# Another order table for the 6,604 calls of a cross-attention kernel

## The chip, the core and the metric

The kernel runs on one core of a Trainium2 chip. Its engines are TensorE (PE; PEld is its weight load), VectorE (DVE), ScalarE (ACT), GpSimd (POOL) and SyncE (SP), which here only issues transfers. The metric is the device time of one execution in microseconds; the median of a few runs is given.

## The reference

Eight batches of 256 rows of width 1024 attend to a context of 256 rows, which serves as keys and as values, with 32 heads of width 32. Everything is float32.

```python
x = (hidden_states - mu) * jax.lax.rsqrt(var + LN_EPS) * ln_gamma + ln_beta
Q = _split_heads(x @ Wq.T)
K = _split_heads(memory_keys)
V = _split_heads(memory_values)
scores = jnp.einsum('bhsd,bhtd->bhst', Q, K) * scale
scores = jnp.where(mask, scores, -jnp.inf)
probs = jax.nn.softmax(scores, axis=-1)
attn = jnp.einsum('bhst,bhtd->bhsd', probs, V)
out = attn.transpose(0, 2, 1, 3).reshape(B, S, HIDDEN) @ Wout.T
return residual + out
```

## The kernel before, in words

**The steps.** Four heads of one batch make a step, so there are 64 steps, n = 0 to 63, eight to a batch. Step n goes through every engine:

- `scores(n)`: 8 matmul calls on PE (tiles `sc`), from the queries (`qa`, `qlo` or a part of `ring`) and the keys `k`. The PSUM pool has four buffers for `sc`, so scores n wait for VectorE to have read scores n-1.
- `softmax_parts(n)`: VectorE adds the mask and takes the minimum (8 calls, tile `e` from `sc`), ScalarE takes the exponentials (8 calls, with the sums `den`), VectorE the reciprocals `rden`; GpSimd, for some tiles ScalarE, scales `e` by them; VectorE transposes four tiles in 32x32 blocks into `pT`. ScalarE copies a part of `pT` aside into `pc`.
- the swaps (`tail` and `swap` in the same function): two transfers `pT<-pT` and then two `pT<-pc`, 128 KB each, put the blocks of partitions in place. SP issues them.
- `values(n)`: 32 matmul calls into `pv`, from `pT` and the values `v_all`. For n = 8 to 53 `values_pair` does two steps at once, 64 calls in a row. In the tables of the profile `pv` is the tile's name.

A matmul call in float32 is two weight loads and two matmuls in PE's stream. So a pair of value runs is 256 instructions, and its matmuls are short: 32 columns of weights on 128.

**The projections.** Between these, PE works on the query projection of a later batch (`pq`; with fewer products of half blocks, `pq_b_P1` to `P7`, for the batches 2 and 3, 4 and 5, 6 and 7) and on the output projection of an earlier one (`po_A`, `po_S`, one product for each of `A11`, `A12`, `A22`, `S1` to `S4`). Sums of weights that those need are kept in DRAM (`kept_T1`, `kept_T3`, `kept_B11`, `kept_B21`) and read back into `ring` or `wq`. `x` is normalized into `xe` and moved in blocks into `xnT`; `r` is the residual. `v_all` has one buffer, `k` two.

**What sets the order.** No scheduler does. The code of `xattn_kernel` is run once against a stand-in, `Recorded` (lines 351 to 371), which writes down each of its 6,604 calls with its engine. Then `nc.issue(ORDER, OTHER)` (line 1606) makes the calls in the sequence that the string `ORDER` (lines 151 to 321) lists by number. Each engine's queue is its own calls in that sequence, and a queue is in order: a call that waits holds everything behind it on its engine. So every instruction in the profile has the line of the call in `issue`, line 367 here, and it is told apart by its tiles. Semaphore waits follow from the data; a PE run placed earlier or later in `ORDER` meets other calls ahead of it, and nothing else changes.

The first transfers stand at the head of SP's queue: `x_0` in four pieces, the slices of `wq` (512 KB each), `x_1` in two (512 KB each), `k`, the mask, `wo` and `v_all`.

Of the kernel before, what the change touches and what calls it, by code (L numbers as in the profile page):

```python
# [151 lines left out]
0-38 41 39-40 47 44 42-43 48 54-57 81 58-77 80 83-88 78-79 94 89-92 95-109 120-123 134 133 93 135 111 110  # L152
112-113 124-130 136-137 114 131 118-119 115-116 138-141 148 142-146 149 147 150-153 156 160-161 132 157 167
158 179-180 162-165 117 159 172 177 181 166 184 168 174 169 176 175 186-187 178 170 182 185 82 171 209 154-155
173 183 189-196 217 188 215-216 223 225 213-214 226 224 218 231 236 229-230 227 237 239 234 287-288 232-233
388 50 45-46 49 197-199 205 200-202 210 203-204 238 228 235 254-261 211 206 212 247 262 207 263-264 274 208
275 265-266 276 488 52 51 219-220 518 243 598 221-222 748 241 240 248 244-246 293-294 250 252 251 280-281 242
249 270 291 253 297-298 278 282 292 279 283 302 295 299 301 300 322 267 277 315 296 323 271 268-269 306 324
328-330 419 307-309 304-305 303 311-314 327 326 331-335 325 372 272 368 273 369 373 370 374-375 371 376-379
414 425 318 320 319 382-383 380-381 310 316-317 336-367 384 321 385 394 396-397 395 400-401 426-427 402-403  # L160
407 398-399 408 411 405-406 409 393 392 410 413 412 404 416 418 417 420 415 422 424 428-430 1236 284-286 53
290 289 421 423 431-478 481 487 387 386 389 391 390 496-497 479-480 482-483 498-499 492 505 500-501 484
506-507 493-495 502 504 503 509 513 515-516 508 517 536-576 581 531-534 582 577 583-585 578 597 486 485 623
510-512 514 524 591-592 521 523 525-526 529 589-590 522 527 519-520 530 611-612 535 593-594 609 605-606
613-614 607 603-604 608 610 615-617 602 601 628 620 625 624 631 641 622 627 621 633 626 632 643-650 579-580
586-588 691-693 619 629 634 694-695 699 635 528 491 490 596 595 489 630 651-690 696 704 709-710 703 705-707
711-712 708 716 718 713-715 725 721 727 618 726 720 719 717 749-756 1235 737 599-600 757-788 741 852 700 697
738 698 850 734 637 809 914 851 702 701 854 636 853 855 735 1598 639 722-723 728 724 747 640 745 793-794
742-744 795-796 789-792 797-800 816-817 801 803 730 733 813 732 731 802 804 820 814-815 805 812 818 821-825
819 826 834 831 827-828 806 729 807 736 638 808 829 836-837 833 832 838-839 642 849 810 739-740 856-897 845  # L170
842-843 830 835 840-841 844 848 898-901 908 906-907 846-847 909 923 938 921-922 919 910 924-925 911-912 811
920 917 926-927 943 930 935 949 932-933 918 931 950 940 953 962-963 746 928-929 937 936 939 941-942 944 946
951 948 947 964 966 902-905 974-981 967-969 1014-1017 982-1013 1028 1032-1035 952 954 1029 965 1038 1036
1026-1027 934 1030 1039 1037 955 1045-1046 945 1043-1044 1047 1040 1055 1050 1068 913 958 915 1079-1086 1166
916 957 1385 970 1018-1025 1048 1042 1049 1041 971 1056 1052-1053 1031 1051 1054 1058 1063 1077 1087-1121
1126-1127 1134 1132-1133 1062 1123 1122 1128 1061 1131 1135 1057 1130 1138 1178-1180 1059-1060 1244 1240 1173
1175 1074 1171 961 1461 1668 1064-1065 1067 956 1072 1066 1129 1136 1139 1137 1148 1143-1144 1140 1142
1145-1147 1149-1150 1141 1152-1155 1151 1157 1160-1161 1073 960 1070 1169 1158-1159 1078 972 1181-1186 1124
1187-1189 1125 1176 1190-1194 1245 1069 1234 1071 1237 959 1460 1199 1197-1198 1200 1203 1195-1196 1162
1205-1207 1209 1212 1201-1202 1210 1228 1211 1213 1204 1156 1251-1322 1387 1208 1218 1215 1217 1216 1177 1224  # L180
1226 1225 973 1335-1336 1214 1323-1326 1337 1219 1221-1222 1163 1165 1164 1220 1241 1167-1168 1243 1338 1340
1345-1346 1229 1327-1329 1343-1344 1227 1349-1353 1223 1230-1231 1233 1232 1359-1361 1247 1356 1347-1348
1354-1355 1357-1358 1362 1366 1374 1242 1379 1239 1238 1388-1395 1330-1334 1383 1396-1398 1407 1368 1370 1369
1372 1408 1373 1367 1399-1406 1413 1363-1365 1249 1248 1250 1667 1375 1371 1376 1378 1409-1410 1415-1416 1446
1377 1172 1449 1424 1419-1421 1411-1412 1417-1418 1414 1450 1422-1423 1341 1425 1451 1430 1427 1431 1426 1433
1342 1432 1339 1436 1440 1437 1441 1438 1452 1463-1536 1588 1439 1592 1174 1170 1381 1596 1428-1429 1434-1435
1459 1386 1454-1455 1462 1246 1545-1546 1553-1554 1551 1442 1543-1544 1555-1556 1552 1564-1565 1443 1557-1563
1566 1568 1567 1457 1456 1589 1569-1573 1547 1575 1577 1576 1593 1599-1606 1537-1542 1594-1595 1607-1608
1621-1622 1549 1578 1625 1619 1627 1617 1582 1634 1623 1636 1632 1665 1865 1380 1445 1444 1382 1574 1580-1581
1448 1447 1579 1609-1613 1618 1620 1624 1635 1626 1633 1628 1583 1638-1639 1076 1640 1663 1629 1642 1644 1550  # L190
1643 1548 1647-1648 1650 1645 1666 1649 1664 1458 1660 1741 1614-1616 1652 1631 1669-1740 1742-1744 1765-1766
1630 1651 1745-1749 1761-1763 1653 1641 1646 1764 1654 1767 1774 1753-1754 1590 1768 1776-1778 1591 1597
1755-1756 1758 1780 1772-1773 1775 1661 1782 1769-1771 1785 1787 1779 1808-1815 1750-1752 1802-1804 1816
1827-1828 1789 1788 1825-1826 1760 1829 1791 1793 1817-1820 1837-1838 1869-1870 1662 1584-1585 1453 1586 1657
1655-1656 1075 1587 1784 1783 1384 1786 1757 1790 1792 1794-1796 1659 1658 1833-1834 1830 1842 1831-1832
1843-1844 1839 1846 1840 1835-1836 1759 1841 1849 1864 1798 1845 1797 1637 1879 1871-1878 1821-1824 1880-1882
2009 1807 1799-1800 1805 1847-1848 1853 1855 1957 1959-1961 1955 1850 1852 1956 1962 1851 1958 1854 2010 1857
1806 1856 1859-1860 1947-1949 1979 1858 1861 1863 1862 1965 1963-1964 1971-1973 1966-1967 1868 1970 1974 1983
1801 1988 2011-2018 1883-1946 1950-1952 1978 1994 1867 1866 1781 2002 2006-2007 1953-1954 2218 2224 2076 1980
1999 1968 1984 1969 1982 1985 1989-1990 1981 2028-2030 1976 1995 2045-2046 1986 2031 1975 1977 1987 1993 1992  # L200
2008 2019 2034 2042 1991 1996-1997 2040 2044 2005 2043 2047-2048 2032-2033 2038 2041 2039 2035 2052-2053 2072
2054-2055 2079-2150 2020-2023 2161 2163-2164 2049 2036-2037 1998 2051 2050 2061 2058 2070-2071 2024-2027 2078
2060 2059 2075 2151-2152 2162 2177 2175-2176 2056 2167 2171-2172 2179 2000 2178 2207 2063-2064 2173-2174 2057
2065 2003 2067 2001 2004 2066 2180 2169-2170 2188 2062 2153-2154 2185 2182-2183 2181 2187 2186 2189 2191-2192
2184 2190 2074 2073 2199 2225-2232 2155-2158 2219-2220 2159-2160 2233-2234 2247 2197 2243 2249-2250 2281
2068-2069 2285 2251-2252 2168 2194 2196 2195 2206 2244 2248 2253-2254 2208 2200 2245-2246 2193 2198 2201 2166
2165 2209 2222 2077 2235-2242 2284 2267 2255 2262 2260 2263 2258 2269 2261 2259 2272 2288-2290 2217 2256-2257
2265-2266 2268 2274 2264 2276 2275 2270 2292 2216 2303-2374 2297 2376-2381 2384 2394-2395 2271 2434 2273 2277
2386-2387 2385 2392-2393 2390 2278 2396 2398-2399 2389 2403-2404 2400 2402 2407-2409 2223 2286 2300 2302 2405
2287 2299 2414 2435-2442 2382-2383 2375 2431 2455-2457 2401 2397 2420 2411-2412 2406 2413 2416-2417 2410 2419  # L210
2428 2418 2433 2301 2221 2443-2444 2432 2445-2450 2453 2458 2454 2429 2461 2470 2422 2451-2452 2462 2468-2469
2472 2466 2459 2474 2485 2463-2464 2473 2465 2298 2497-2499 2574-2575 2573 2501-2508 2576-2581 2626 2211 2210
2202 2491 2291 2295 2421 2212 2204 2215 2280 2214 2296 2294 2203 2293 2213 2494 2479 2496 2475 2687 2490 2279
# [1433 lines left out]
```

## Time and profile before

| | us |
|---|---|
| median of 3 runs | 572.59 (571.46 to 572.81) |
| the profiled execution's own time | 572.86 |
| its span, first to last instruction | 571.1 |
| PE busy | 559.8 |
| VectorE, ScalarE, GpSimd busy | 463.8, 441.4, 402.5 |
| mean granted TensorE clock | 0.997 |

How to read the profile: a row of the timeline is a run of like instructions, with its start and its length in us, and in brackets the idle time before it with what ended that. In a row of windows stands, behind the stretch and its length, the busy time and the count of instructions of PE, PEld, DVE, ACT and POOL, then the granted clock, the share of the DMA engines and GB/s. A group's row ends in its busy time, the mean in ns of one, and the idle time before its instructions. "issue" is idle time that ended on nothing that the profile shows. The DMA queue q8 carries TensorE's instructions; q1 the transfers that SP issues.

### The profile page before, as it was taken

What the parts mean: (1) busy time and instruction counts of PE and PEld (TensorE: products, weight loads), DVE (VectorE), ACT (ScalarE), POOL (GpSimd) and SP (SyncE); (2) the same over time, 40 slices, a digit from 0 to 9 for tenths busy, and PEclk for the clock granted to TensorE, in tenths of its full rate; (3) what the DMA queues carried; (4) which work ended last, traced back from release to release, by engine and by line L of the source; (5) the groups of instructions that cost most, each with busy time, mean ns of one, the idle gap of its engine ahead of it and who ended that gap; (6) DMA issues with size and microseconds to landing.
All of it is one profiled execution on the core that took longest, in us unless ns stands there. A gap on an engine that the chain in (4) does not pass through costs nothing.

```text
span 571.1 us, 18695 instructions
## 1 busy us (share of the span) xinstructions
PE 559.8 (98%) x6586; PEld 374.2 (66%) x6586; DVE 463.8 (81%) x1709; ACT 441.4 (77%) x1475; POOL 402.5 (70%) x633
## 2 busy tenths in 40 slices
PE   8999999999999999999999989999999999899997
PEld 7787776676666766767666656666766666555544
DVE  6799898898798979887898958887777788788824
ACT  3599998798886687978877858887869758898930
POOL 1579898989978684679967783378865776366781
PEclk9999999999999999999999989999999999999999
DMA  8988874887567877877667767687665755665443
GB/s 303 365 229 235 232 196 112 223 245 222 166 183 232 222 200 207 226 211 200 174 174 228 207 177 225 167 232 190 170 176 152 208 152 145 190 200 142 131 113 129
DMA packets 46477, 112.64 MB, mean 197 GB/s; under 512 B 9008, under 2 KB 9776, under 8 KB 46384
## 3 DMA queue, kind: packets, MB, share of 16 engines
q1 hardware_dynamic: 40384, 91.52, 56.7%
q0 software_dynamic: 5712, 19.93, 11.6%
q8 instruction: 52, 0.85, 0.6%
q14 instruction: 41, 0.34, 0.2%
q10 hardware_dynamic: 288, 0.01, 0.0%
HBM read 58.99 MB, written 12.58 MB: 125 GB/s over the span
## 4 chain that ended last, share of the span: by engine, by line
PE 88%; DMA 4%; DVE 3%; ACT 3%; issue 1%; SPq 0%; ACTq 0%; DVEq 0%
PE pq_P L367 25%; PE po_S L367 19%; PE sc L367 11%; PE pv L367 11%; PE po_A L367 10%; PE pq L367 8%; PE po_end L367 3%; ACT e L367 2%; DMA wq<-in_wq_dram 2%; PE po_last L367 1%; DMA pT<-pc 1%; DVE e L367 1%; DMA pT<-pT 1%; DVE pT L367 1%; DMA bet<-in_beta_dram 1%
## 5 line engine op out<-in xcount | busy, mean ns | idle before, releaser
L367 ACT ACTIVATE e<-e,mn 128x256 f32<-128x256 f32 x512 | 255.8, 501 | 53.7 <-DVE mn L367 44.0
L367 POOL TENSOR_SCALAR e<-e,rden 128x256 f32<-128x256 f32 x408 | 190.4, 480 | 127.7 <-DVE rden L367 119.4
L367 DVE CUSTOM_DVE_ANT_0 e<-sc,mb 128x256 f32<-128x256 f32 x512 | 191.7, 411 | 12.8 <-PE sc L367 9.5
L367 DVE STREAM_TRANSPOSE pT<-e 128x512 f32<-128x512 f32 x256 | 175.2, 699 | 30.1 <-POOL e L367 21.2
L367 PE MATMUL pq_P<-xnT,wq 128*128 128x256 f32 x544 | 133.4, 386 | 2.7 <-issue 2.6
L367 PEld LDWEIGHTS pq_P<-xnT,wq 128*128 128x128 f32 x544 | 102.0, 191 | 45.2 <-issue 29.9
L367 ACT ACTIVATION_READ_ACCUMULATOR e<-e,mn 128x1 f32 x512 | 96.9, 189 | 0.0
L367 ACT COPY pc<-pT 128x512 f32<-128x512 f32 x128 | 76.9, 611 | 15.1 <-DVE pT L367 9.6
L367 PE MATMUL po_S<-wo,at 128*128 128x512 f32 x152 | 73.1, 603 | 0.0
L367 DVE RECIPROCAL rden<-den 128x2 f32<-128x2 f32 x256 | 37.4, 153 | 34.2 <-ACT e L367 32.5
L367 PE MATMUL pv<-pT,v_all 64*32 64x128 f32 x3584 | 61.4, 273 | 2.7 <-DMA pT<-pc 1.5
L367 PE MATMUL pq<-xnT,wq 128*128 128x256 f32 (+3 forms) x272 | 61.0, 373 | 0.9 <-ACT xnT L367 0.8
L367 PEld LDWEIGHTS pv<-pT,v_all 64*32 64x32 f32 x3584 | 51.6, 105 | 14.7 <-issue 9.3
L367 PE MATMUL po_A<-wo,at 128*128 128x512 f32 x128 | 60.2, 600 | 0.0
L367 ACT ACTIVATE e<-e,rden 128x256 f32<-128x256 f32 x104 | 49.8, 502 | 11.8 <-DVE rden L367 11.7
L367 PEld LDWEIGHTS pq<-xnT,wq 128*128 128x128 f32 x272 | 47.7, 190 | 10.5 <-issue 2.2
L367 PE MATMUL po_S<-wo,s 128*128 128x512 f32 x104 | 50.1, 599 | 0.0
L367 PE MATMUL sc<-k,qa 32*128 32x256 f32 x640 | 48.5, 402 | 0.3 <-DVE mn L367 0.3
L367 PEld LDWEIGHTS po_S<-wo,at 128*128 128x128 f32 x152 | 28.6, 192 | 22.7 <-issue 19.8
L367 PEld LDWEIGHTS sc<-k,qa 32*128 32x128 f32 x640 | 30.6, 184 | 18.7 <-issue 8.0
L367 DVE DVE_READ_ACCUMULATOR2_ANT mn<- 128x1 f32 x512 | 42.2, 82 | 0.0
L367 ACT COPY at<-pv 128x128 f32<-128x128 f32 x128 | 30.4, 252 | 14.4 <-PE pv L367 13.0
(97 smaller groups left out, 601.2 us busy)
## 6 DMA issues: line engine op xcount, KB each, us to landing
pT<-pT SPq DMA_DIRECT2D x128, 128.0 KB, 3.0
pT<-pc SPq DMA_DIRECT2D x128, 128.0 KB, 3.9
v_all<-in_kv_dram POOLq DMA_DIRECT2D x17, 512.0 KB, 4.9
k<-in_kv_dram SPq DMA_DIRECT2D x30, 256.0 KB, 3.8
r<-in_x_dram SPq DMA_DIRECT2D x26, 256.0 KB, 3.7
xnT<-xe SPq DMA_DIRECT2D x92, 64.0 KB, 3.3
out_dram<-r POOLq DMA_DIRECT2D x18, 256.0 KB, 3.9
wq<-in_wq_dram SPq DMA_DIRECT2D x8, 512.0 KB, 8.9
```

The costliest lines, as they stand in the source:

```text
L367: getattr(getattr(self.nc, other.get(i, engine)), name)(*a, **k)
```

## The change

`ORDER` is replaced: 170 lines of numbers before, 169 after, so that line 367 becomes 366. The calls, the plan, the tiles and buffers are the same, and `OTHER` stays empty. The table's first lines:

```diff
 ORDER = """
-0-38 41 39-40 47 44 42-43 48 54-57 81 58-77 80 83-88 78-79 94 89-92 95-109 120-123 134 133 93 135 111 110
...
 """
 OTHER = {}
```

Three places show it as queues. The first is PE behind the values of the pair 34/35 (`pv_34`), to the first scores of step 39. `pq_4_P7` is a product of the query projection for batches 4 and 5, `po_3_S2` one of the output projection for batch 3. Before:

```order
L367 MATMUL pv_34_1_1207<-pT_35_1124,v_all_115 32x128
L367 MATMUL pq_4_P7_1179<-xnT_5_844,wq_120 128x256 x3
L367 MATMUL po_3_S2_1143<-wo_126,at_3_1_1046 128x512
L367 MATMUL pq_4_P7_1179<-xnT_5_844,wq_120 128x256 x3
L367 MATMUL sc_39_0_1227<-k_38_1142,qa_119 128x256
```

After:

```order
L366 MATMUL pv_34_1_1207<-pT_35_1124,v_all_115 32x128
L366 MATMUL pq_4_P7_1179<-xnT_5_844,wq_120 128x256 x7
L366 MATMUL po_3_S2_1143<-wo_126,at_3_1_1046 128x512
L366 MATMUL pq_4_P7_1179<-xnT_5_844,wq_120 128x256
L366 MATMUL sc_39_0_1227<-k_38_1142,qa_119 128x256
```

Four more `pq` calls stand directly behind the value run. Counted over PE's whole queue, the run begins 9 instructions earlier against a multiple of 256 than it did. At the pair 8/9, two of the four `po_0_S2` calls that followed the run now precede it.

The second place is SP's queue around the swaps of step 36 (tiles `pT_36`, `pc_36`), which are issued while PE is at that pair. Before:

```order
L367 DMA r_3_1_0_1116<-in_x_dram 128x512
L367 DMA pT_36_1151<-pT_36_1151 32x1024
L367 DMA xnT_6_1174<-xe_6_1061 32x512
L367 DMA pT_36_1151<-pT_36_1151 32x1024
L367 DMA k_40_1198<-in_kv_dram 128x512
L367 DMA ring_105<-kept_T3_123 128x1024
L367 DMA xnT_6_1174<-xe_6_1061 32x512 x2
L367 DMA pT_36_1151<-pc_36_1152 32x1024
L367 DMA xnT_6_1174<-xe_6_1061 32x512 x3
L367 DMA pT_37_1180<-pT_37_1180 32x1024 x2
L367 DMA pT_36_1151<-pc_36_1152 32x1024
```

After:

```order
L366 DMA k_40_1198<-in_kv_dram 128x512
L366 DMA pT_36_1151<-pT_36_1151 32x1024
L366 DMA xnT_6_1174<-xe_6_1061 32x512
L366 DMA pT_36_1151<-pT_36_1151 32x1024
L366 DMA r_3_1_0_1116<-in_x_dram 128x512
L366 DMA xnT_6_1174<-xe_6_1061 32x512
L366 DMA pT_37_1180<-pT_37_1180 32x1024 x2
L366 DMA pT_36_1151<-pc_36_1152 32x1024 x2
L366 DMA xnT_6_1174<-xe_6_1061 32x512
L366 DMA pT_37_1180<-pc_37_1181 32x1024 x2
```

The 512 KB move `ring<-kept_T3` that stood between the swaps of step 36 is gone from here (it is issued earlier, ahead of the swaps of step 30), and so are most of the `xnT` moves between the swaps, which come in two blocks of five ahead of them; `r_3_1_0` comes a little later and `wq<-kept_B11` now stands behind the swaps of step 37.

The third is the head of SP's queue, the first transfers of the kernel. Before:

```order
L367 DMA x_0_127<-in_x_dram 128x512 x4
L367 DMA wq_120<-in_wq_dram 128x1024
L367 DMA x_1_130<-in_x_dram 128x1024
L367 DMA k_0_128<-in_kv_dram 128x512
L367 DMA mk_0_129<-in_mask_dram 128x512
L367 DMA k_2_131<-in_kv_dram 128x512
L367 DMA wq_120<-in_wq_dram 128x1024 x2
L367 DMA x_1_130<-in_x_dram 128x1024
L367 DMA v_all_115<-in_kv_dram 128x512
L367 DMA wo_126<-in_woT_dram 128x2x512
L367 DMA x_2_214<-in_x_dram 128x1024
L367 DMA wq_120<-in_wq_dram 128x1024 x3
```

After:

```order
L366 DMA x_0_127<-in_x_dram 128x512 x4
L366 DMA wq_120<-in_wq_dram 128x1024
L366 DMA k_0_128<-in_kv_dram 128x512
L366 DMA mk_0_129<-in_mask_dram 128x512
L366 DMA wq_120<-in_wq_dram 128x1024
L366 DMA x_1_130<-in_x_dram 128x1024
L366 DMA wq_120<-in_wq_dram 128x1024 x2
L366 DMA x_1_130<-in_x_dram 128x1024
L366 DMA wq_120<-in_wq_dram 128x1024 x2
L366 DMA wo_126<-in_woT_dram 128x2x512 x2
L366 DMA k_2_131<-in_kv_dram 128x512
L366 DMA v_all_115<-in_kv_dram 128x512
```

The first half of `x_1` moves behind the keys, the mask and a second slice of `wq`; `k_2` and `x_2` move back, and `wo` and the slices of `wq` change places. On VectorE the four statistics calls of `x_1` then stand ahead of the second half of step 0's scores.

Beyond these, calls of the projections move from one gap between scores and values to another: behind scores 41 there are 16 `pq` and 12 `po` calls until its values, before 22 and 13; at step 21 it is 24 and 9, before 38 and 12; at step 0 33 `pq`, before 46; at step 53 28 and 10, before 26 and 9; at step 54 24 and 12, before 24 and 8.

More of the change, by code (lines that the diff above doesn't have):

```diff
@@ L157 @@
[L157 to L161, printed above, removed]
@@ new lines @@
+221-222 285 284 286 336-367 325 372-373 368-370 374-375 371 376-379 396 394-395 382-383 380 397 381 392-393
+425 321 384 400-401 398-399 317 402 404 407-408 385 411 413 403 412 426 405-406 410 416-417 420 415 422 427
+418 428 430-438 471-478 481 479 496 494 498 597 289-290 388 421 424 482 423 409 480 483 488 386-387 53 487 391
+390 497 495 499-501 507 502-506 429 508 484-486 509 518 513 524 510-512 514 525-526 515 517 529 536-544
+439-470 528 489-491 531-533 535 581 534 577 582 578 583 579-580 589 521 519 523 516 522 590 605-606 530 493
@@ new lines @@
+492 545-576 591-593 520 616 527 594-596 603-604 609 614 607-608 610-613 615 618 602 617 601 628 620-622
+624-625 627 626 635 643-650 584-588 651-682 693-694 619 683-685 691-692 629-631 623 699 599-600 707 713-714
+634 708 704 715 741 686 742 687-688 749 852 700 1078 633 632 695-696 698 703 705-706 709 718-719 710 716-717
+711-712 721 724 730 732 750-788 689-690 743-744 789 801 725 727 726 854-855 697 809 738 734 737 739 637 702
+701 849 853 971 745 722-723 639-640 728 803-804 731 720 793-794 790-791 795 792 796-800 802 814-816 729 805
@@ new lines @@
+4044 4233 4241 4275 4284 4282 4277 4290 4295 4297 4296 4310 4247 4110-4111 4249 4294 4303 4244 4314-4317
+4319-4390 4392 4401-4402 4285 4292 4391 4393-4400 4403-4404 4291 4411 4299 4409-4410 4298 4300 4412 4405 4408
+4415 4420 4413 4424 4422-4423 4407 4417 4421 4416 4406 4426 4425 4418-4419 4431 4433 4427 4437 4414 4439
+4434-4435 4445 4243 4250 4242 4452 4454 4301 4453 4246 4302 4245 4307 4313 4457-4464 4456 4465-4466 4479
+4477-4478 4438 4467-4474 4480-4482 4428 4430 4429 4255 4440 4451 4490-4491 4432 4475-4476 4492 4436 4487 4489
```

306 lines of the change are left out of this document (148 added, 158 removed).

## The prediction

> **What bounds the kernel now.** I read the page first: engine shares and the granted clock, and then what the chain that ended last is made of.
>
> ```profile
> PE 559.8 (98%) x6586; PEld 374.2 (66%) x6586; DVE 463.8 (81%) x1709; ACT 441.4 (77%) x1475; POOL 402.5 (70%) x633
> PE 88%; DMA 4%; DVE 3%; ACT 3%; issue 1%; SPq 0%; ACTq 0%; DVEq 0%
> q8 instruction: 52, 0.85, 0.6%
> ```
>
> TensorE (PE) is busy for 98% of the span, and the chain runs through it for 88%. The same matmuls are issued before and after, so an order can only win back holes, or open new ones. Next I read what PE itself waited for, in the table of waits.
>
> ```profile
> PE pq_P L367 <- issue: 2.6, 2, 2.1
> PE pv L367 <- DMA pT<-pc: 1.5, 2, 0.9
> PE pv L367 <- issue: 1.1, 2, 0.5
> ```
>
> Two kinds count: 2.6 + 1.1 = 3.7 us on "issue", when nothing that the profile shows held PE up, and 1.5 us in which values calls waited for the last swaps. The timeline places the largest hole.
>
> ```profile
> 330.37 2.03 PE L367 MATMUL pv<-pT,v_all 64*32 64x128 f32 x128
> 332.33 0.92 PE L367 MATMUL pq_P<-xnT,wq 128*128 128x256 f32 x3
> 335.34 1.48 PE L367 MATMUL pq_P<-xnT,wq 128*128 128x256 f32 x3 [2.09 <-issue]
> 143.63 0.66 PE L367 MATMUL pv<-pT,v_all 64*32 64x128 f32 x28 [0.53 <-issue]
> 418.68 0.59 PE L367 MATMUL pq_P<-xnT,wq 128*128 128x256 f32 x2 [0.53 <-issue]
> 453.03 0.64 PE L367 MATMUL pv<-pT,v_all 64*32 64x128 f32 x24 [0.53 <-issue]
> ```
>
> All four lie inside, or just behind, a pair of value runs: 128 matmuls and as many weight loads in 2.03 us, 256 instructions. What do they wait for? Counting PE's instructions between them answers it.
>
> ```profile
> 143.60:335.30 191.70, 189.58 (x2269) 126.43 (x2268) 165.57 (x606) 151.02 (x499) 146.12 (x235) 1.00 0.72 203
> 335.30:418.65 83.35, 82.81 (x1005) 55.84 (x1006) 62.38 (x236) 64.20 (x220) 51.85 (x85) 0.98 0.69 190
> 418.65:453.00 34.35, 33.82 (x378) 21.47 (x378) 27.68 (x108) 27.75 (x95) 21.39 (x37) 1.00 0.67 187
> ```
>
> The first two counts are PE's matmuls and weight loads. With the semaphore waits that stand between them (71, 37 and 12 by the difference), the stretches are 18, 8 and 3 times 256 instructions. PE's queue q8 carried 52 packets, 0.85 MB / 52 = 16 KB each, for 13,172 instructions and those waits: about 256 to a packet. So the four holes are packets that came late: numbers 11, 29, 37 and 40 in my count. A value pair spends a whole packet in 2 us; a run of `pq_P` takes about 0.215 us a matmul and its load, some 27 us a packet. The DMA view says why number 29 was the worst; first 329 to 332.8 us, then 332.8 to 334.2.
>
> ```profile
> q1 hardware_dynamic: 415, 1.04, 98.2%
> ring<-kept_T SPq DMA_DIRECT2D x1, 512.0 KB
> ```
>
> ```profile
> q1 hardware_dynamic: 145, 0.25, 70.4%
> q8 instruction: 1, 0.02, 5.4%
> ```
>
> For 3.8 us the data queue filled the DMA engines and no instruction packet moved; it moved when they came free, and PE started 1.1 us after that window. The hole then cost more than its length:
>
> ```profile
> 333.30:335.30 2.00, 0.00 (x0) 0.00 (x0) 1.72 (x10) 2.00 (x8) 1.68 (x4) 1.00 0.69 112
> 335.30:338.40 3.10, 3.06 (x6) 1.77 (x7) 0.71 (x3) 1.79 (x9) 1.82 (x3) 0.54 0.88 271
> ```
>
> The granted clock was 0.54 for the next 3.10 us: 3.10 x (1 - 0.54) = 1.4 us lost. Packet 29 cost 2.1 + 1.4 = 3.5 us.
>
> The Trainium skill ("TensorE: Matmul & The Clock Gate", Part 1: The HAM clock gate) puts half clock behind an idle window of about 3.4 us, free-running. By that a hole of 2.1 us should not bring it, and filling the hole would win 2.1, not 3.5; the sum below would be 1.4 higher, 571.0. The trace differs: 0.54 directly after 2.0 us of nothing.
>
> **The change, part by part.** The sum is made against the profiled execution, 572.86 us, a span of 571.1 and 1.8 outside it; the median of the runs is 572.59, 0.3 lower.
>
> *Packet 29 (pair 34/35).* The pair starts 9 instructions earlier in its packet. Between the pair's end and the packet's first instruction stood 3 `pq_P` matmuls (0.65 us start to start); now stand 7, 1.51 us. Between the point where the packet seems to be asked for (256 instructions ahead of its first) and that first instruction PE has 3.54 us of work, before 2.76. SP's 512 KB `ring<-kept_T` no longer stands ahead of pT_36's second swaps. At the rate above (1.04 MB in 3.8 us) that is 1.9 us of transfers. The packet took 335.34 - 330.5 = 4.8 us from there; less 1.9 it is 2.9, under 3.54: no hole, 3.5 us won. If the transfers are no help, the hole is 4.8 - 3.5 = 1.3 us: 2.2 won at full clock, 0.8 at half. I take -3.0 (-3.5 to -0.8).
>
> *Packets 11, 37, 40.* Each hole is 0.53 us, 1.6 in all. PE's work in the same stretch goes from 4.9 to 4.8, 2.1 to 2.6 and 4.3 to 2.8 us; the last pair also begins 15 instructions earlier, so the supply may be asked for sooner or later. I take -1.0 (-1.6 to 0).
>
> *Packet 8 (pair 8/9).* This one was safe, because of what followed the pair:
>
> ```profile
> 106.93 2.11 PE L367 MATMUL pv<-pT,v_all 64*32 64x128 f32 x128
> 109.07 3.67 PE L367 MATMUL po_S<-wo,s 128*128 128x512 f32 x8
> ```
>
> Some 3.0 us of work lay between run and packet. Two of those four calls now stand ahead of the run, so 1.3 us is left, and the run sits where 34/35 sat. No row shows this place under another order. Nearest are packet 11's hole (0.53) and packet 29's with its clock (3.5), which had twice the DMA load. I take +1.0 (0 to 3.5).
>
> *The waits for swaps at 53 and 54.* Their rows, with the swap on the chain:
>
> ```profile
> 487.00 1.13 PE L367 MATMUL pv<-pT,v_all 64*32 64x128 f32 x62 [0.88 <-DMA pT<-pc]
> 489.53 6.42 DMA pT<-pc
> 496.08 1.36 PE L367 MATMUL pv<-pT,v_all 64*32 64x128 f32 x64 [0.65 <-DMA pT<-pc]
> ```
>
> The order puts 2 `pq` and 1 `po` calls more between scores 53 and its values, 4 `po` calls more at 54. A call is two matmul records: 2 x 0.215 = 0.43 us for `pq`; from the row at 109.07, (112.58 - 109.07) / 8 x 2 = 0.88 for `po`.
>
> ```profile
> 112.58 1.46 PE L367 MATMUL pq_P<-xnT,wq 128*128 128x256 f32 x6
> ```
>
> That is +1.7 and +3.5 us, over the 0.88 and 0.65 waited: -1.5 (-1.6 to -0.5, if the chains lengthen as well).
>
> *Distance taken elsewhere.* Step 41, with what its last swap showed; the pT view is 374 to 386 us:
>
> ```profile
> 355.95 1.21 PE L367 MATMUL sc<-k,qlo 32*128 32x256 f32 x16
> L367 SPq DMA_DIRECT2D pT<-pc x2: 507/507/507, 375.8 to 377.7; - x2
> DMA to landing us min/median/max: 3.4/5.3/6.0
> 383.62 2.10 PE L367 MATMUL pv<-pT,v_all 64*32 64x128 f32 x128
> ```
>
> The swap of 377.7 landed at about 377.7 + 5.3 = 383.0; step 41 is the second half of the pair and starts near 384.5. So it had 1.5 us to spare. Behind scores 41 the order now has 6 `pq` and 1 `po` calls fewer, -3.4 us: a wait of 2.0 if the chain is no shorter. Step 0 is read the same way (swaps 33.6 to 34.2, 3.1 us to landing):
>
> ```profile
> pT<-pc SPq DMA_DIRECT2D x2, 128.0 KB, 3.1
> 43.19 1.16 PE L367 MATMUL pv<-pT,v_all 64*32 64x128 f32 x64
> ```
>
> It had 43.2 - 36.7 = 6.5 to spare and loses 13 `pq` calls, 5.6. But VectorE's queue now has the whole of the second x tile's statistics and more, some 4 us, ahead of step 0's last transpose: a wait of up to 3.1. Pair 20/21 loses 14 to 16 `pq` and 3 `po` calls, about 9 us, with 6.4 us to spare at step 21:
>
> ```profile
> pT<-pc SPq DMA_DIRECT2D x2, 128.0 KB, 2.3
> 218.25 1.01 PE L367 MATMUL pv<-pT,v_all 64*32 64x128 f32 x54
> ```
>
> (issued up to 210.4, landed by 212.7, second half at 219.1). The wait is 2.2 with an unshortened chain. But between scores 21 and its swaps the order has less work: VectorE's falls from 14.3 to 10.1 us and ScalarE's alike, counted from the order by the means of the page (0.41 and 0.70 us for VectorE's two commonest), which more than covers 2.2:
>
> ```profile
> L367 DVE CUSTOM_DVE_ANT_0 e<-sc,mb 128x256 f32<-128x256 f32 x512 | 191.7, 411 | 12.8 <-PE sc L367 9.5
> L367 DVE STREAM_TRANSPOSE pT<-e 128x512 f32<-128x512 f32 x256 | 175.2, 699 | 30.1 <-POOL e L367 21.2
> ```
> Steps 41 and 0 have partial cover of that kind. In all 0 to 2.0 + 2.2 + 3.1 = 7.3; I take +0.5.
>
> *The start.* The second weight slice was on the chain:
>
> ```profile
> 6.12 8.70 DMA wq<-in_wq_dram
> 14.87 1.14 PE pq L367 x4
> GB/s 303 365 229 235 232 196 112 223 245 222 166 183 232 222 200 207 226 211 200 174 174 228 207 177 225 167 232 190 170 176 152 208 152 145 190 200 142 131 113 129
> ```
>
> In SP's queue it now stands behind one more 512 KB slice and one 256 KB k less: 256 KB at 303 GB/s, 0.8 us. I take +0.7 (0 to 2.0, as other loads are reordered too).
>
> The sum: 572.86 - 3.0 - 1.0 + 1.0 - 1.5 + 0.5 + 0.7 = **569.6 us**.
>
> **The rivals.**
>
> *The packets come late all the same.* The worst runs hardly move against their packets: 34/35 by 9 instructions of 256. With the lost cover at packet 8 and 40 the loss could only change its place. Then only the swap waits go: 572.86 - 1.5 = 571.4. Against it: the 512 KB that kept packet 29 out is gone from there.
>
> *The distance taken away is missed (slower).* Place: values of 0, 21 and 41. At full price 7.3 us, and packet 8 and the start 1.7, against 5.5 won: 572.86 + 3.5 = 576.4. It decides from the point where those chains stay as long as they were (25.9 us from scores 41 to its last swap's landing, 27.1 at step 21) and packets give only half of their gain. For it: swaps took 5.3 us here, and 6.4 at step 54, so a short chain can still land late. Against: less work stands on VectorE and ScalarE at step 21.
>
> *The holes are not instruction supply.* The hole at 333 could be something that the profile doesn't show and that stays where that work is. All four stay, and with the swap waits gone, the start and the distance it is 572.86 - 1.5 + 0.7 + 0.5 = 572.6. The Trainium skill ("Runtime: NRT & Kernel Launch", Instruction fetch mechanics) says this much: blocks of 256 instructions are fetched while the current one runs, and the cost is "mostly hidden" because dispatch is slower than the fill. The trace speaks against it: distances of 18, 8 and 3 blocks between holes, and the q8 packet moving only in the hole.
>
> **How the numbers follow.** Two measurements of this kernel can be told apart from about 0.3%, 1.7 us: faster is under 570.9, slower over 574.3. The forecast has a chance of 0.55 (its own range is 566 to 571.5: the terms' good ends give 572.86 - 6.7 + 0 = 566), the first rival 0.18, the slower one 0.2, the third 0.07. Faster: nearly all of the forecast (0.5) and a third of the first rival (0.06), 0.56. Slower: most of the slower rival (0.18) and what packets 8 and 40 could cost in the first (0.04), 0.22. Same: the rest. The range leaves out a tenth at each end: 565.5 to 576.
>
> **What would show it.** The table of waits: `pv <- DMA pT<-pc` gone at 53/54, and no new one at 0, 21 or 41. The "issue" rows: none over 1 us, no slice near 330 at half clock, nothing over 0.6 behind pair 8/9. The first `sc` of step 1 within 1 us of before's. The forecast is wrong if a hole of over 2 us, on issue or on pT, stands anywhere, or if PE's busy time grows.

## The result, and the profile after

The changed kernel takes **563.41 us** (median of 4 runs, 562.63 to 564.35), the one before 572.23 (4 runs, 571.46 to 572.81): a ratio of 0.9847, 95% interval 0.9824 to 0.9871, so 8.8 us less. The prediction was 569.6, with a range of 565.5 to 576.0: the direction was right, the size was not, and the time lies below the range. The profiled execution took 564.11 us with a span of 562.2, so 1.9 us lie outside it (before: 1.8).

The page's engine row, and the table of what PE itself waited for:

```profile
PE 556.1 (99%) x6586; PEld 371.7 (66%) x6586; DVE 461.7 (82%) x1709; ACT 441.5 (79%) x1475; POOL 403.0 (72%) x633
```

```profile
PE busy L366 <- POOL ring masks.py:199: 1.3, 1, 1.3
PE po_S L366 <- DVE rden L366: 0.5, 1, 0.5
PE pv L366 <- DMA pT<-pc: 0.4, 2, 0.2
PE pq L366 <- ACT xnT L366: 0.4, 1, 0.4
PE pq L366 <- DMA wq<-in_wq_dram: 0.3, 1, 0.3
PE po_S L366 <- issue: 0.2, 1, 0.2
```

The 3.7 us on "issue" have become 0.2, at one place. The pair 34/35, where PE stood still for 2.1 us, on the timeline of after, with the stretch behind it in the windows:

```profile
326.43 2.10 PE L366 MATMUL pv<-pT,v_all 64*32 64x128 f32 x128
328.46 3.29 PE L366 MATMUL pq_P<-xnT,wq 128*128 128x256 f32 x14
331.59 1.02 PE L366 MATMUL po_S<-wo,at 128*128 128x512 f32 x2
```

```profile
325.00:330.00 5.00, 5.00 (x153) 3.96 (x153) 4.80 (x16) 2.65 (x7) 2.39 (x6) 1.00 0.54 145
328.40:332.00 3.60, 3.60 (x24) 2.96 (x16) 2.95 (x16) 3.51 (x13) 1.61 (x4) 1.00 0.66 178
```

No row has a bracket: no hole, the clock at 1.00, and the DMA engines 0.54 busy where before they were full. PE's busy time fell as well, by 3.7 us, though it does the same matmuls. Part of that is the half clock. The other part is waits that never show as idle time, which the prediction missed. This is step 11's scores on PE, first before, then after:

```profile
96.95 0.71 PE L367 MATMUL sc<-k,qa 32*128 32x256 f32 x6
97.94 1.13 PE L367 MATMUL sc<-k,qa 32*128 32x256 f32 x10 [0.28 <-DVE mn L367]
105.22 1.78 PE L367 MATMUL sc<-k,qa 32*128 32x256 f32 x16
```

```profile
95.10 1.15 PE L366 MATMUL sc<-k,qa 32*128 32x256 f32 x16
103.26 1.15 PE L366 MATMUL sc<-k,qa 32*128 32x256 f32 x16
```

Sixteen score matmuls take 1.15 us. Before, those of step 11 took 97.94 + 1.13 - 96.95 = 2.1 and those of step 12 1.78, so 0.9 and 0.6 too long, yet the table of PE's waits has only 0.3 us on `mn`: the wait stood at the weight load, whose row in the table for PEld reads, before and then after:

```profile
PEld sc L367 <- DVE mn L367: 8.8, 16, 0.8
```

```profile
PEld sc L366 <- DVE mn L366: 5.7, 12, 0.8
```

Most of these 8.8 us are not lost, since the weight loads wait while earlier matmuls still run: after has 5.7 of them left and almost no late scores. What is lost shows in the length of the rows of 16 `sc`.

To account for all of it I took each run of like matmuls from its start to the next run's start, less its matmuls at their steady rate (0.2155 us for `pq`, 0.4285 for `po`, 0.0675 for `sc`, 0.0169 for `pv`). What is left over is the excess, which sums to 28.2 us before and 19.4 after, 8.9 less, as the spans (571.1 and 562.2):

| excess, us | before | after |
|---|---|---|
| the first 45 us | 6.4 | 5.8 |
| late packets and half clock (before at 141, 250, 332 to 340, 416, 451; after at 108) | 6.6 | 0.5 |
| scores that wait for VectorE (97, 105, 220, 229; after 339) | 2.2 | 0.25 |
| values that wait for swaps (485, 494; after 393 and 395) | 1.8 | 1.3 |
| a `po` call that waits for a sum (after at 374) | 0 | 0.7 |
| all other changes from one kind of matmul to another (294 and 296) | 11.3 | 10.9 |

### The profile page after: what moved, and what is told of

Read it like the earlier page. It is cut to its first block, busy times and chain, and to the rows that moved or that the text cites. A ratio compares the mean times of both kernels' runs of the same rounds, so it can differ in the third digit from the quotient of the medians.

```text
span 562.2 us, 18707 instructions
## 1 busy us (share of the span) xinstructions
PE 556.1 (99%) x6586; PEld 371.7 (66%) x6586; DVE 461.7 (82%) x1709; ACT 441.5 (79%) x1475; POOL 403.0 (72%) x633
## 4 chain that ended last, share of the span: by engine, by line
PE 88%; DMA 6%; SPq 2%; DVE 1%; POOL 1%; issue 0%; ACT 0%; DVEq 0%; POOLq 0%
PE pq_P L366 24%; PE po_S L366 18%; PE sc L366 11%; PE pv L366 11%; PE pq L366 10%; PE po_A L366 10%; DMA pT<-pT 4%; PE po_end L366 3%; SPq L366 2%; DMA pT<-pc 1%; PE po_last L366 1%; DMA x<-in_x_dram 1%; PE po_end_s L366 0%; PE px L366 0%; POOL e L366 0%
## 5 line engine op out<-in xcount | busy, mean ns | idle before, releaser
L366 PE MATMUL pq_P<-xnT,wq 128*128 128x256 f32 x544 | 131.4, 382 | 0.0
L366 PE MATMUL sc<-k,qa 32*128 32x256 f32 x640 | 47.1, 401 | 0.0
```

What stands on the lines that cost most here:

```text
L366: getattr(getattr(self.nc, other.get(i, engine)), name)(*a, **k)
```

## The experiments

Every kernel is the order before or the order after with the edit shown. Times are medians; before was run beside them, with medians of 572.0 to 573.0. The theory: PE's packets of 256 instructions come late where a pair of value runs lies at a certain place in its packet and transfers are ahead in the DMA engines. The rivals: the gain comes from the places of the transfers alone, or from the place of the runs alone, or the holes have another cause.

**b_pad60: the same order, shifted against the packets by 60 instructions.**

```diff
+    for _ in range(30):
+        nc.nc.tensor.transpose(busy[:32, :32], ident[:32, :32], ident[:32, :32])
     nc.issue(ORDER, OTHER)
```

> The order before, with 30 transposes of 32 x 32 put ahead of PE's first instruction: 60 instructions, which shift every later one against the packets of 256 and change nothing else (about 1 us at the start, where PE waits for x anyway). Theory (packet supply): the four holes on issue, at 143, 333, 418 and 453 us, vanish with the half clock, 4 to 5 us; new holes of 0.3 to 2.5 us each stand behind the pairs that the shift brings to the same place in a packet, 28/29 (279 us), 38/39 (368 us) and 50/51 (470 us), and at no other. In all from 4 us faster to 2 us slower. Rival (the holes come from the transfers or the work at those times): all four stay within 0.5 us where they were and nothing new opens; the time is that of before, up to 1 us more.

Measured: 571.49 us (568.29 to 576.05), ratio 0.9986 (0.9953 to 1.0019); the profile is of the execution of 576.05. The four holes are gone, and with them the half clock at 335: no bracket stands at 143, 333, 418 or 453. One large new hole opened, on the timeline:

```profile
383.01 2.11 PE L374 MATMUL pv<-pT,v_all 64*32 64x128 f32 x128
385.05 0.70 PE L374 MATMUL po_S<-wo,s 128*128 128x512 f32 x1
388.67 1.69 PE L374 MATMUL po_S<-wo,s 128*128 128x512 f32 x3 [2.92 <-issue]
```

It stands behind the pair 40/41. I had named 38/39; I had read the place on a count of PE's work and set it against the clock of the trace one pair too early, and the same slip makes 28/29 of 30/31. Of the three places so meant, one has a hole. So the holes moved with the packets and not with the work or the transfers at their times: the rival falls. The time did not follow: the pad cost some 2 us at the start, and in the profile waits for swaps rose to 3.5 us and one of 1.4 us on ScalarE opened at 54.

**a_shift32: the order after, shifted back by 32 instructions.** 16 of the first 32 transposes, which only keep PE busy, are left out.

```diff
-0-38 ...
+16-38 ...
```

> The order after, with 16 of the 32 transposes that only keep TensorE busy at the start left out (they compute nothing that is used): every PE instruction stands 32 earlier against the packets. Theory (packet supply): five value pairs come to the place where the order before had its holes: the pairs 12/13, 18/19, 26/27, 34/35's neighbour 38/39 and 46/47 (packets 11, 16, 24, 32, 40); holes on issue of 0.3 to 2.5 us behind most of them, the time 2 to 7 us longer than after. Rival (the new order's gain is that of its transfers): no hole, the time within 1 us of after.

Measured: 570.86 us (567.30 to 572.95), ratio to before 0.9986 (0.9959 to 1.0013), where after has 0.98; the profile is of an execution of 572.84. This is the clearest run: no call of the order moved, and 7.4 of the 8.8 us were lost (against 563.41, measured at another time; before stood at 572 both times). The timeline at two of the places, and the clock there:

```profile
194.62 2.02 PE L374 MATMUL pv<-pT,v_all 64*32 64x128 f32 x127
198.89 0.29 PE L374 MATMUL pv<-pT,v_all 64*32 64x128 f32 x1 [2.26 <-issue]
280.03 2.03 PE L374 MATMUL pv<-pT,v_all 64*32 64x128 f32 x128
283.28 1.02 PE L374 MATMUL pq_P<-xnT,wq 128*128 128x256 f32 x4 [1.22 <-issue]
367.46 0.70 PE L374 MATMUL po_A<-wo,at 128*128 128x512 f32 x1
369.98 0.76 PE L374 MATMUL po_A<-wo,at 128*128 128x512 f32 x1 [1.82 <-issue]
```

```profile
194.00:203.00 9.00, 6.74 (x158) 4.33 (x154) 5.22 (x24) 5.89 (x20) 5.44 (x7) 0.81 0.68 183
365.00:373.00 8.00, 6.18 (x148) 4.44 (x141) 6.34 (x24) 6.70 (x23) 3.58 (x8) 0.83 0.51 114
279.00:285.00 6.00, 4.78 (x152) 3.76 (x152) 4.62 (x16) 3.64 (x13) 1.91 (x4) 1.00 0.48 138
```

Packets 16, 24 and 32 came late as counted, 40 by 0.4 us, 11 not (the pairs of 24 and 40 were again named one too early: they are 28/29 and 48/49). A late packet that had not been counted cost 1.0 us at 488. Holes and half clock at the counted places make 9.5 us of excess, against 0.5 in after. The start adds little: PE stands idle for 1.9 us in place of the transposes, until x comes, and its clock falls once, but the run of 32 `pq` that starts at 66.92 us in after and at 67.35 in its repeat starts at 67.61 here.

**b_early_ring: one transfer moved in the order before.**

```diff
 SP's queue
+ring<-kept_T3          (call 3694, 512 KB)
 pT_30<-pT_30 ...
 pT_36<-pT_36 x2, k_40
-ring<-kept_T3          (call 3694, 512 KB)
 xnT<-xe x2, pT_36<-pc_36
```

> The order before, with one transfer moved: the 512 KB ring<-kept_T that SP issued between the swaps of step 36 (at 329 us) is issued ahead of the swaps of step 30. PE's own queue is that of before. Theory (instruction packets that have to queue behind transfers): packet 29's hole behind the pair 34/35 (2.1 us, and 3.1 us at a clock of 0.54) shrinks to at most 1 us with little or no half clock, the packet lands 1 to 2 us sooner; the time falls by 2 to 3.5 us, and the three holes of 0.53 us at 143, 418 and 453 stay. Rival (only the place of the value run in its packet counts): the hole stays at 2 us or more and the time within 1 us of before.

Measured: 570.34 us (568.74 to 575.61), ratio 0.9985 (0.9950 to 1.0019). The hole is shorter and the half clock is gone; the excess there fell from 4.25 to 1.8:

```profile
332.57 0.92 PE L374 MATMUL pq_P<-xnT,wq 128*128 128x256 f32 x3
334.88 0.91 PE L374 MATMUL pq_P<-xnT,wq 128*128 128x256 f32 x3 [1.39 <-issue]
```

```profile
335.00:338.40 3.40, 3.40 (x19) 2.40 (x23) 0.89 (x3) 2.33 (x11) 1.57 (x3) 1.00 0.90 269
```

The missing half clock is no proof of the theory. In b_waits, further down, PE's queue up to this place and the transfers are those of before, and the clock stayed at 1.00 behind a hole of 1.86 us:

```profile
334.83 0.92 PE L374 MATMUL pq_P<-xnT,wq 128*128 128x256 f32 x3 [1.86 <-issue]
334.85:338.26 3.41, 3.41 (x19) 2.41 (x23) 0.45 (x3) 1.97 (x10) 1.95 (x3) 1.00 0.88 275
```

So the transfer is worth 0.5 to 0.7 us of the hole, from one execution each, and not the 1 to 2 us expected; 1.4 us were left. Elsewhere two other packets cost more than in before (0.8 us of excess at 250 and 1.4 at 449, against 0.3 and 0.8). The time's interval includes no change.

**b_pv_first: one run moved in the order before.**

```diff
 PE's queue
+pv_34 (64 calls)
 sc_38 (8 calls)
-pv_34 (64 calls)
 pq_4_P7 x3, po_3_S2
```

> The order before, with one run moved on PE: the values of the pair 34/35 are issued ahead of the scores of step 38 instead of behind them, 32 instructions earlier in the same packet, so that 1.1 us of scores stands between the run and the packet's end; the transfers are those of before. Theory (packet supply): the hole shrinks from 2.1 by about 1 us, the half clock behind it may go (1.4 us); the time falls by 1 to 2.5 us. Rival (only the load of the transfers counts): the packet arrives when it arrived, so the hole shrinks by no more than the 1.1 us of scores and the clock stays at half: at most 1 us. Rival (no instruction supply at all): the hole moves with the run and keeps its 2.1 us.

Measured: 570.18 us (569.03 to 572.97), ratio 0.9984 (0.9961 to 1.0007). The hole fell to 0.34 us at full clock:

```profile
332.00 0.92 PE L374 MATMUL pq_P<-xnT,wq 128*128 128x256 f32 x3
333.26 0.92 PE L374 MATMUL pq_P<-xnT,wq 128*128 128x256 f32 x3 [0.34 <-issue]
```

That is 1.75 us less than in before, and 1.5 less than in b_waits, for 1.1 us of scores behind the run. The place of the run alone does most of it, with all transfers where they were; the rival "transfers only" allowed at most the 1.1 us. The margin is small, and it is the shifts, which move no transfer, that refute this rival. In the same profile a hole of 1.24 us stands at 419 and a wait of 1.68 at 402; the time's interval includes no change.

**a_late_ring: the 512 KB put back into the order after.**

```diff
 SP's queue
-ring<-kept_T3          (ahead of pT_30<-pT_30)
 pT_36<-pT_36 x2
+ring<-kept_T3
 r_3_1_0, xnT<-xe
```

> The order after, with one transfer put back: the 512 KB ring<-kept_T is issued between the swaps of step 36 again, as before, and not ahead of the swaps of step 30. PE's own queue is that of after. Theory (packets queue behind transfers): packet 29 comes 1 to 2 us later and a hole of 0.5 to 2.5 us opens behind the pair 34/35, perhaps with half clock behind it: 0.5 to 4 us slower than after. Rival (the new place of the run covers it): no hole over 0.5 us there, within 1 us of after. A late product that needs this ring half would show apart, as a wait on the transfer.

Measured: 564.12 us (563.52 to 565.73), ratio 0.9842 (0.9793 to 0.9891): after, within its spread, and no hole at 34/35. But SP issued the move at 329.2 us, behind the packet of a run that had started at 326.3, so it was never ahead of it. The run does not tell the theories apart.

**b_waits: the other waits taken out of the order before.**

```diff
 VectorE's queue
-ring<-wq sum (call 1668)  ahead of the last reads of scores 10
+ring<-wq sum (call 1668)  behind them
-wo<-wo sum (call 1460)    ahead of the reads of scores 11
+wo<-wo sum (call 1460)    behind them
 PE's queue
+po_5_S1 x2, pq_6_P7
 pv_52 (64 calls)
-po_5_S1 x2, pq_6_P7
+po_5_S1 x2
 pv_54 (32 calls)
-po_5_S1 x2
```

> The order before, with the waits that are not packets taken out: two sums of weights on VectorE (ring<-wq at 93 us, 2.35 us long, and wo<-wo at 101 us, 1.1 us) are issued behind the last reads of scores 10 and 11 instead of ahead of them, and two po calls and one pq call are issued ahead of the values of 52/53, two po calls ahead of those of 54. Theory (scores wait for VectorE, values for swaps): the excess of the scores at 97 and 105 us (0.97 and 0.63) and that of the values at 485 and 494 us (1.05 and 0.71) falls to 0.2 or less each; 2 to 3.4 us faster than before, the holes on issue at 143, 333, 418 and 453 as before. Rival (those waits only hide the next late thing): less than 1 us.

Measured: 571.10 us (568.24 to 572.49) against 572.95, ratio 0.9956 (0.9929 to 0.9983): about 2 us. All four waits went, and others of 0.7 us opened at 399 and 492; scores 11 and 12, and values 52/53, on PE:

```profile
96.92 1.15 PE L374 MATMUL sc<-k,qa 32*128 32x256 f32 x16
104.22 1.15 PE L374 MATMUL sc<-k,qa 32*128 32x256 f32 x16
485.81 2.10 PE L374 MATMUL pv<-pT,v_all 64*32 64x128 f32 x128
```

The holes stayed (2.2 us of excess at 332, without the half clock). So what made the scores late was a VectorE sum in front of their reads; in the order before it stood there, 2.35 us long:

```profile
93.23 2.35 DVE L367 TENSOR_TENSOR ring<-wq 128x512 f32<-128x512 f32 x1
```

**a_start: the order after with the first loads as before.**

```diff
 SP's queue
 x_0 x4, wq
+x_1, k_0, mk, k_2, wq x2, x_1, v_all, wq x3
-k_0, mk, wq, x_1, wq x2, x_1, wq x2
 wo x2
```

> The order after, with the head of SP's queue as before: x_1's first half ahead of the keys, k_2 ahead of the second slice of wq, and the slice that after loads early behind v_all. First theory (mine on record: the new order of the loads costs 0.7 us, one slice of wq coming later): 0.5 to 1 us faster than after, the first 45 us shorter. Rival (what the trace of after showed, 0.6 us less excess in the first 45 us): 0.3 to 2 us slower, with a wait on wq in the first 20 us.

Measured: 563.92 us (563.40 to 564.20), ratio 0.9867 (0.9821 to 0.9912). The excess of the first 45 us is 6.6; in the other profiles of the order after it is 5.8 to 6.4, in those of before 6.2 to 6.5. The head of SP's queue is worth 0.2 to 0.8 us of excess by these profiles, in favour of the new order, and nothing that the times show. My term of +0.7 is not borne out.

**a_mend8 and a_mended: the order after, with the waits that its profile shows taken out.** a_mend8 is the first of the three edits alone.

```diff
 PE's queue
-po_0_S2 x2                 both kernels
 pv_8 (64 calls)
+po_0_S2 x2
-po_4_S2                    the rest in a_mended only
 sc_44 (8 calls)
+po_4_S2
+pq_6_P5 x4                 (and the GpSimd sum of xnT_7 ahead of them)
 pv_42 (64 calls)
-pq_6_P5 x4
```

> The order after, with the two po calls that it issues ahead of the values of 8/9 put back behind them. Theory (packet 8 comes late because only 1.3 us of work is left behind the run; 0.2 and 1.7 us of hole in two profiles of after): no hole at 108 to 112 us, 0.3 to 1.7 us faster than after. Rival (8 instructions are too few to matter, or the values then wait): within 0.3 us of after.

> The order after, with the waits that its own profile shows taken out: two po calls go back behind the values of 8/9 (hole of 0.5 us in packet 8), one po call that waits for a sum at 374 us (0.5) goes behind the scores of step 44, and four pq calls, with the GpSimd sum that they need, go ahead of the values of 42/43, which waited for their swap (1.3 us). Theory: each of the three goes, 1.5 to 2.5 us faster than after. Rival (each wait only hands on to another, or the shifts of 8 to 16 instructions bring another value pair to the bad place): within 0.7 us of after or slower.

Measured: a_mend8 562.85 us (562.30 to 563.02, 4 runs), ratio 0.9847 (0.9802 to 0.9892). The hole of packet 8 in the repeat of after below, and the same place in a_mend8:

```profile
108.71 1.55 PE L374 MATMUL po_S<-wo,s 128*128 128x512 f32 x3
111.96 0.59 PE L374 MATMUL po_S<-wo,s 128*128 128x512 f32 x1 [1.70 <-issue]
```

```profile
105.24 2.14 PE L374 MATMUL pv<-pT,v_all 64*32 64x128 f32 x128
107.31 3.70 PE L374 MATMUL po_S<-wo,s 128*128 128x512 f32 x8
```

No hole there (one of 0.45 us opened at 414), and the lowest time of the study, some 0.6 us under after and its repeat, which were timed apart from it. a_start, timed beside it, has 1.2 us of excess at packet 8 and took 563.40 to 564.20 us, outside a_mend8's 562.30 to 563.02; its other difference, the first loads, is not separated from this. a_mended took 567.88 us (566.29 to 569.58), 4 us more than after: the product put ahead of 42/43 was not ready and stood for 1.4 us, a later one for 1.0 on its `xnT`, and the waits at 374 and 393 that it was to cure are not in the repeat of after at all. They were of that one execution.

**a_again: the order after, once more.**

> The order after, unchanged, beside the other kernels of this call on the same chip. Both theories: 1.2 to 1.9% faster than before, and in its profile no hole over 0.6 us on issue and no half clock.

Measured: 563.58 us (563.04 to 564.81), ratio 0.9826 (0.9785 to 0.9867). The excess is 19.5 us: 2.0 at packet 8, 0.4 at 414, and none of the waits for swaps or sums of the first profile.

**b_shift24: the order before, shifted by 24 the other way.** 12 of the first 32 transposes are left out.

```diff
-0-38 ...
+12-38 ...
```

> The order before, with 12 of the 32 transposes that only keep TensorE busy at the start left out (they compute nothing that is used): every PE instruction stands 24 earlier against the packets, and no call moves. Theory (packet supply): the pairs 34/35, 44/45, 12/13, 48/49 and 26/27 leave the bad place; the holes on issue at 333 (with its half clock), 418, 143, 453 and 250 us go, and only the pair 14/15 (166 us) comes to it, 0.3 to 2 us. Holes fall from 6.6 to 2 us or less. The start costs 1 to 2 us, because PE stands idle before x is ready and its clock falls, as the run with 16 left out showed. In all 2 to 5 us faster than before. The waits for scores and swaps stay. Rival (the new order's gain is in the places of its calls and transfers): holes as before, 1 to 2 us slower.

Measured: 571.78 us (570.65 to 574.68), ratio 0.9994 (0.9961 to 1.0027). The packets did as counted: the holes at 250, 333, 418 and 453 are gone, 0.3 us of excess is left at 141, and the pair 14/15 has one (1.1 us at 169); a hole of 0.9 us in the pair 16/17 was not foreseen. From 6.6 us the excess of packets fell to 2.9. The time did not fall by as much: in the profile the waits ahead of values at 314, 401 and 485 make 2.4 us more than those of before, and the start 0.6 more, so that the excess fell by 1.0 us and the median by 0.4, within the noise. In the table of PE's waits those for swaps rose to 2.5 us, from 1.5; the second row holds the 1.14 us at 401, which is no packet:

```profile
PE pv L374 <- DMA pT<-pc: 2.5, 2, 1.4
PE pv L374 <- issue: 2.4, 4, 1.1
```

**b_both and b_both2: that shift and more distance together.**

```diff
-0-38 ...
+12-38 ...
 the moves of b_waits, and
+pq_2_P5 x5     ahead of pv_14   (b_both)
+po_3_S2 x2     ahead of pv_32   (b_both; in b_both2 pq_4_P3 x2)
+pq_6_P5 x3     ahead of pv_42   (b_both)
```

> The order before, with both cures together: the shift of 24 instructions (12 of the transposes that only keep TensorE busy left out), and more distance: the two VectorE sums behind the reads of scores 10 and 11, and pq or po calls put ahead of the values of 14/15 (five, which also brings that run past the bad place), 32/33 (two), 42/43 (three), 52/53 (three) and 54 (two). Theory (the two cures need each other: where packets no longer hold PE up, values reach their swaps too soon): the waits of 1.1 us or more that stood at 314, 401, 485 in the run with the shift alone go, and holes stay under 1.5 us in all, so 4 to 6 us faster than before in spite of 1.9 us that the start costs: 566 to 568. Rival (the two cures add up as measured alone, 1.0 and 0.4 us): 570 to 571.

> As the run before it, without the edits that put calls in front of values that were not ready themselves: the order before with the shift of 24 instructions, the two VectorE sums behind the reads of scores 10 and 11, three calls ahead of the values of 52/53, two ahead of those of 54, and two pq calls ahead of those of 32/33. Theory (the two cures need each other): against the run with the shift alone the waits at 98, 106, 314 and 485 us (0.71, 0.64, 1.28, 1.65) go, the holes of 1.4 and 1.1 us at 167 and 176 and the wait at 400 stay: 3 to 4 us less than that run, 567.5 to 569, and at least 1 us less than with the same moves without the shift. Rival (the cures add up as measured alone): 570 to 571. Rival (each wait hands on to the next): 571 or more.

Measured: b_both 579.99 us (574.20 to 590.95), ratio 1.0086 (1.0035 to 1.0137). It tells nothing of the theory: a product moved ahead of 42/43 waited for 5.0 us, with half clock over 6.8 us, and calls at 172 and 315 waited 1.3 and 0.9 for their operands. b_both2 571.93 us (567.68 to 577.40), ratio 0.9979 (0.9940 to 1.0017). The waits it was to cure are gone from its profile (scores at 98, swaps at 314 and 485), but a late packet at 167 (2.1 us of excess, a hole of 1.72) and waits at 75 and 398 to 401 (3.5 us in all) stand in their place. My expectation that the two cures need each other, and would then bring 3 to 4 us, did not come true; each wait handed on to the next.

## Why the prediction was wrong in its size

Term by term, in excess of the profiled executions:

| term | predicted | measured |
|---|---|---|
| packet 29, pair 34/35 | -3.0 | -4.25 |
| packets 11, 37, 40 | -1.0 | -2.0 |
| packet 21 (250 us) | not listed | -0.3 |
| packet 8, pair 8/9 | +1.0 | +0.5 (0 to 2.0 in four profiles) |
| swaps at 53 and 54 | -1.5 | -1.8 |
| distance taken elsewhere | +0.5 | +1.3 at 42/43, 0 in the repeat |
| the start | +0.7 | -0.6 (-0.6 to 0 in the profiles of after) |
| scores that wait for VectorE | not listed | -2.0 |
| a sum waited for, and all small changes | not listed | +0.3 |
| sum | -3.3 | -8.9 |

Of the 5.6 us missed, the packets are 2.5, the scores 2.0 and the start 1.3; packet 8 and the swaps add 0.8, the distance and the small changes take 1.1 away.

**What held.** The mechanism: holes that are late packets, at multiples of 256 instructions, and longer where little work is left behind the run. The shifts show it with no call moved, so a call placed elsewhere changes more than what stands ahead of a run. The traces show it once more when PE's matmuls, weight loads and semaphore instructions are counted together: every hole put down to a packet ends at instruction 193 or 194 of a block of 256, counted from 0. In before these are the instructions 3265, 7874, 9921 and 10689, in a_shift32 4546, 6593 and 8641, in b_pad60 9154, in the repeat of after 2497. The "issue" waits at 401 in b_shift24 and at 406 in b_both end at 11 and 13 of a block: they are something else.

The packets' own times say how. At these holes 2.2 to 3.1 us passed from the start of a packet's move to PE's first instruction out of it, and a pair takes 2.03 us, so at 418 in before a hole of 0.53 us opened though the packet moved 0.35 us after the instruction 256 ahead of its first. Packet 29 moved 2.5 us after that instruction in before, 2.3 in b_waits, 1.9 in b_early_ring and 0.14 in after. That the rest of this delay is the other transfers fits DMA engines that were 98% busy; no run shows it alone.

Packet 8 was put at +1.0 and costs 0 to 2; a_mend8 removes it by giving back the work behind the run. The Trainium skill ("Runtime: NRT & Kernel Launch", Instruction fetch mechanics) calls the crossing of a block "mostly hidden". Here its blocks of 256 are right and that word is not: one shift of 32 instructions was worth 7 us, at most 0.7 of it at the start.

**The step that failed** is the list of terms: the waits of scores stood at nothing. "Next I read what PE itself waited for, in the table of waits", the prediction says, and it took its terms from the two kinds in that table. That table counts idle time of the matmuls alone. Scores that wait at their weight load were in PEld's table (8.8 us on `mn`) and in rows of 16 `sc` that last 1.8 or 2.0 us where 1.15 is normal. Two microseconds were missed so, and b_waits shows for 1.6 of them that a VectorE sum ahead of the reads makes them. The new order has those sums elsewhere. The start failed too: +0.7 was forecast for one slice of weights, and between 0 and 0.6 us were won.

**Mis-sized:** the packets. For 29 the sum took 3.0 of a price of 3.5, and 4.25 went; for the small ones 1.0 of 1.6, and 2.0 went. So 1.1 us were given away for fear that a lost cover would keep part of each, while none of them cost more than 0.4 in any profile of after; the rest was priced too low. A hole of 0.53 us in the table is 0.5 to 0.8 in excess, since the matmuls around it run less tightly too, and the half clock lasted 3.41 us (1.7 lost) and not 3.10 (1.4). The 1.9 us credited to the moved 512 KB were 0.4 to 0.6 by b_early_ring; no run shows which of the other moves brought the packet in time. Nor had packet 29 twice the DMA load of the places beside which it was set: the share of the DMA engines is 0.98 at 329 to 332.8 us, and 1.03 at 140.9 to 143.1 and at 106.9 to 109.1.

**Luck** lies in the half clock. The price of packet 29 was read from an execution that had it. Of 83 executions of before that were timed beside the experiments, 38 have a clock under 0.999 (median 573.5 us) and 45 have not (571.1); none of the 12 named at the end for the order after has.

**The distances** at 0, 21 and 41, the slower rival, cost nothing; that VectorE and ScalarE had less to do there is argued, not measured. A wait opened at 42/43 in one execution, which no sum had named. The rivals that packets come late all the same, and that the holes are something else, fall with the timeline of after and the shifts.

**What stays open** is why the same cures, put into the order before one by one or together, bring 2 us at most and not 8.8 (b_both lost 8). Even those 2 are in part the clock: among executions at 0.999 or more, the medians of b_early_ring, b_pv_first and b_waits lie 0.8, 0.6 and 0.3 us below before's. In each of those kernels the cured wait is gone from the trace or shorter, and another wait, mostly for swaps, is there. I have not shown what the new order does to have none of them; that all its distances were made together is only an argument.

## What to carry to other kernels

Where a run of short matmuls spends a whole packet of 256 instructions in 2 us, its place in the packet matters: count instructions, leave long matmuls behind the run (behind the pair 8/9, 3.0 us left no hole, and 1.3 us left holes of up to 1.7), and recount after every edit, since two calls moved elsewhere shift all that follows. Read waits of PE from the weight loads and from rows that last longer than their kind, not from PE's idle time alone. A single cure in a full schedule often buys only the next wait, so price the sum at what the whole excess could be, and keep the range as wide.

## What the runs showed that I had not expected

The clock halves behind short holes, and the length of the hole does not decide it alone. The lower clocks above are means over the windows shown; each is half clock for 3.41 us, as here in before:

```profile
335.55:338.96 3.41, 3.41 (x7) 2.02 (x7) 0.46 (x3) 1.54 (x8) 2.38 (x4) 0.50 0.87 260
```

In each trace with records of the clock such a stretch starts a whole number of steps of 3.413 us after the first record of the clock (in before 331.09 us, 97 steps). So I divided each profiled execution into these steps and added up PE's idle time in each. Behind a step with 1.82 us or more of it, half clock followed: 1.82 and 2.26 us in a_shift32, 2.09 in before, 2.12 (of the hole of 2.92) in b_pad60. Behind a step with less than 1.70 it never did, though two holes were longer: the 1.86 us of b_waits fell into two steps with 1.22 and 0.64, and a wait of 2.00 us in b_pad60, at 314, with 0.45 and 1.55. At 1.70 itself, half a step, it did once (the start of b_shift24) and once not (the repeat of after). So the same hole can cost 1.7 us more in one execution than in the next. The Trainium skill ("TensorE: Matmul & The Clock Gate", Part 1: The HAM clock gate) gives a free-running window of about 3.4 us, and half clock after an idle one. The steps here agree with the window; none of them was idle throughout, not even at the wait of 5.0 us in b_both (2.63 and 2.41).

The order before also scatters more: 569.0 to 574.6 us in 31 executions timed together, and up to 578.1 at other times, where 12 of the order after (its own, the repeat, and the one with the late transfer) stay within 562.6 to 565.7. Those of before that have a half clock are 2.4 us slower in the median than the others. Packets that come late by luck of the transfers would do the rest; no run was made to show it.
